# A six-block latent transformer on one core: the first group's order, products of zeros ahead of it, norms' deviations as powers on GpSimd, and two stores issued earlier

## Chip, core and metric

One core of a Trainium2 chip. The core has a matmul engine (TensorE, PE in the profile; its weight loads are PEld), VectorE (DVE), ScalarE (ACT), GpSimd (POOL) and SyncE (SP), which issues most DMAs. Each engine works through its own queue in order; semaphores tie the queues together. The metric is the device time of one launch in microseconds, the median of several runs. All data is float32.

## What is computed

There are 64 sequences of 32 tokens with 256 features, 2048 tokens in 16 tiles of 128, and a context of 257 rows of 64 features per sequence. Six blocks follow one another, each added to the residual:

```python
x = x + _L0_xattn_ref(_layernorm(x), ctx_512, Wq, Wkv_expand, Wout)   # causal, 16 heads of 16; the first 32 context rows matter
x = x + _L0_attn_ref(_layernorm(x), g_norm, Wq, Wkv, Wout, g_out)     # 16 heads of 128, one key head, l2-normed q and k
x = x + _L0_ffn_ref(_layernorm(x), Wr, br, W1, W2)                    # gelu, best 4 of 16 blocks of each token
x = x + _L1_xattn_ref(_layernorm(x), ctx_512, ...)                    # latent cross attention over 257 rotated keys
x = x + _L1_attn_ref(_layernorm(x), Wq, bq, Wk, bk, Wv, bv)           # causal, grouped keys
x = x + _L1_ffn_ref(_layernorm(x), router_w, gate_w, up_w, down_w)    # best one of 8 experts
```

A layer norm is `(x - mean) / sqrt(var + 1e-5)`. The kernel needs `1 / sqrt(var + eps)` for each token, and the second block has a norm of a norm.

## The kernel before

The residual stays on the chip in 16 tiles `xs[t]`; four tiles make a group `g`, and most projections are done for a group (512 columns) at a time. The six blocks are six stages with pools of their own, which reuse one another's space on the chip, so a buffer of a new stage can have to wait until the old stage's last readers, DMAs among them, are done. The stages are named a to f. In every stage PE's order is the program's order (`manual_schedule`); in stage b this holds for DVE, ACT and POOL too, in stage c for ACT. Where an engine is not listed, a planner with a cost model sets its order by when it thinks the operands are ready, and SyncE's DMA issues are ordered by the planner throughout.

**Norms.** `stats` (L141) takes mean and variance on DVE. `rstd_of` (L131) makes the reciprocal deviation in three steps: add eps on DVE (L134), square root on ACT (L136), reciprocal on DVE (L138). `ln_group` (L146) does four tiles; with `twice` it calls `rstd_of` a second time for the norm of a norm; it ends with the shift (L161) and the scaling of the four tiles, on DVE (L171) or ACT (L167). Square root belongs to another function table of ACT than exp or gelu, so a load of a table stands wherever the kind changes. Names of norms: a, b, r and c (the routing and the hidden layer of the third block), d, e, f (the last block's routing, `route_norm`, L1533).

**The start of stage a.** SyncE issues the constants (L72: 1214 columns, among them the identity for turning tiles, two masks, and at the end cosines and sines of the rotation), then the tiles 0 to 3 of x, the weights of a, the context of group 0, further x and contexts, then the weights of later stages. `group(g, part)` (L347) makes the features of a group in three parts: part 0 norms and turns the latents (`transposed`), part 1 makes the queries, part 2 the keys from the context (`ctxa`, L369), which ACT writes in four masked copies (L377). For group 0 the parts run in the order 2, 0, 1 (L445), then `score(0)` (L384). For tiles t = 0 to 17 the loop at L457 then runs the scores of t + 1, the output of t - 2, the values of t + 1 and so on, with one part of the next group per tile.

**Stage b** goes tile by tile; on every second t, `rotate` (L624) rotates a tile of the context on POOL and stores it for stage d. `rotate_last` (L654) does so for the last, 257th, key of all sequences: five small loads, three products and sums on POOL, and a store to `lkd` (L671). It stands at t = NT = 16, the loop's last turn (L913).

**Stage c** computes the hidden layer (`hidden`, L558, gelu on ACT; `output`, L572) of groups 1 to 3, and between them merges the weights of the fourth block. In its last group, each of four steps i does an output tile, a part of stage d's first queries (`d_queries`, L1047), and `last_out(i)` (L1019), which computes the last key's part of the output, copies it to `zs`, which lies in the space of the weight d_q, and after each second call stores half of it to `zd` with two DMAs (L1031). Products of `d_queries` and `last_out` share two PSUM buffers ("w").

**Stage d** starts with `score(0)`: PE (L1235), maximum on DVE (L1243, `nm`), exp on ACT (L1247, into `pp`), product on DVE (L1256). Its pool reuses the space of stage c's weights.

**Stage e** runs per tile: scores on PE (L262), mask and maximum on DVE, subtraction on POOL (L217), exp on ACT, turn on PE (L230), values spread on POOL (`vde`, L1498), output on PE (L1510), x added on POOL (L1524). The norms of groups e2 and e3 and the five norms of the routing f lie in it, and POOL also stores the rows of each expert (L1615). **Stage f** then computes 23 tiles of expert rows.

Of the kernel before, what the change touches and what calls it, by code (L numbers as in the profile page):

```python
# [7 lines left out]
F32 = mybir.dt.float32  # L8
# [5 lines left out]
P = 128  # L14
# [31 lines left out]
def perceiver_kernel(ctx: ExitStack, tc: tile.TileContext, a: dict, out: bass.AP):  # L46
# [17 lines left out]
    def weight(pool, name, shape):  # L64
        return pool.tile(shape, F32, name=name)
# [3 lines left out]


    cst = const.tile([P, C_N], F32, name="cst")
    nc.sync.dma_start(cst, a["consts"])  # L72
    xf = [const.tile([P, DP], F32, tag=f"x{t}", name=f"x{t}") for t in range(NT)]
    xs = [x[:, :D] for x in xf]
    for t in range(4):
        nc.sync.dma_start(xs[t], a["x"][t * P : (t + 1) * P, :])
    a_q = weight(wap, "a_q", [P, KC, D])

    a_kv = weight(wap, "a_kv", [P, 2 * D])
# [28 lines left out]
        nc.sync.dma_start(xs[t], a["x"][t * P : (t + 1) * P, :])  # L108
    for g in range(1, NG):
        load_ctxa(g)  # L110

    ident = cst[:, C_ID : C_ID + P]
    blk = cst[:, C_BLK : C_BLK + P]
# [8 lines left out]
    srt = dram.tile([NR, DP], F32, name="srt")  # L122
    ones = const.tile([P, S], F32, name="ones")
    nc.vector.memset(ones, 1.0)
    qeps = const.tile([P, 1], F32, name="qeps")
    nc.vector.memset(qeps, 1e-12 / 4096.0)
    keps = const.tile([P, 1], F32, name="keps")
    nc.vector.memset(keps, 1e-12 / 16.0)


    def rstd_of(mv, n, name):  # L131

        ve = sm(f"lnv_{name}", [P, n])
        nc.vector.tensor_scalar_add(ve, mv[:, :, 1], EPS)  # L134
        sd = sm(f"lns_{name}", [P, n])
        nc.scalar.activation(sd, ve, AF.Sqrt)  # L136
        rs = sm(f"lnr_{name}", [P, n])
        nc.vector.reciprocal(rs, sd)  # L138
        return rs
# [3 lines left out]
        nc.vector.bn_stats(st, src)  # L143
        nc.vector.bn_aggr(mv_slot, st)

    def ln_group(g, name, twice=False, act=False):  # L146

        mv = sm(f"lnm_{name}{g}", [P, 4, 2])
        for i in range(4):
            stats(mv[:, i, :], xs[4 * g + i], f"{name}{g}_{i}")  # L150
        rs = rstd_of(mv, 4, f"{name}{g}")
        if twice:

            v2 = sm(f"lnw_{name}{g}", [P, 4, 2])
            nc.vector.tensor_tensor(v2[:, :, 1], mv[:, :, 1], rs, ALU.mult)
            nc.vector.tensor_tensor(v2[:, :, 1], v2[:, :, 1], rs, ALU.mult)
            rs2 = rstd_of(v2, 4, f"{name}{g}b")
            nc.vector.tensor_tensor(rs2, rs2, rs, ALU.mult)
            rs = rs2
        sh = sm(f"lnh_{name}{g}", [P, 4])  # L160
        nc.vector.scalar_tensor_tensor(sh, mv[:, :, 0], -1.0, rs, ALU.mult, ALU.mult)  # L161
        xn = []
        for i in range(4):
            y = xnp.tile([P, D], F32, tag="xn", name=f"xn_{name}{g}_{i}")
            x_ = xs[4 * g + i]
            if act:
                nc.scalar.activation(  # L167
                    y, x_, AF.Identity, scale=rs[:, i : i + 1], bias=sh[:, i : i + 1]
                )
            else:  # L170
                nc.vector.scalar_tensor_tensor(  # L171
                    y,
                    x_,
                    rs[:, i : i + 1],
                    sh[:, i : i + 1].to_broadcast([P, D]),
                    ALU.mult,
                    ALU.add,
                )
            xn.append(y)
        return xn  # L180
# [98 lines left out]
    kvp = wb0.enter_context(tc.tile_pool(name="wB0", bufs=2))  # L279

    def keys_norm(g):
        latT[g] = ln_group(g, "b", twice=True, act=True)

    def keys_turn(g, ps):
        latT[g] = transposed(latT[g], ps, g, "b", gain=gn)
# [41 lines left out]
    with tc.tile_pool(name="wA", bufs=2) as work, tc.tile_pool(  # L327
# [19 lines left out]
        def group(g, part):  # L347

            if g >= NG:
                return  # L350
            if g not in feats:
                qT = work.tile([P, KC, 512], F32, tag="qT", name=f"qTa{g}")
                kd = work.tile([P, KC, 16, 2, S], F32, tag="kd", name=f"kda{g}")
                feats[g] = [qT, kd, None]
            if part == 0:
                feats[g][2] = transposed(ln_group(g, "a"), ps2, g, "a")
            qT, kd, xT = feats[g]
            for o in range(KC):
                osl = slice(o * P, (o + 1) * P)
                if part == 1:  # L360
                    q_ps = ps2.tile([P, 512], F32, tag="mm", name=f"qa{g}_{o}")
                    for k in range(KC):
                        nc.tensor.matmul(
                            q_ps, a_q[:, k, osl], xT[:, k, :], start=(k == 0), stop=(k == KC - 1)
                        )
                    nc.scalar.copy(qT[:, o, :], q_ps)
                if part == 2:
                    k_ps = ps2.tile([P, 512], F32, tag="mm", name=f"ka{g}_{o}")
                    nc.tensor.matmul(  # L369
                        k_ps,  # L370
                        a_kv[0:DC, osl],
                        ctxa[0:DC, 4 * g : 4 * g + 4, :],
                        start=True,
                        stop=True,
                    )
                    for w in range(2):
                        nc.scalar.activation(  # L377
                            kd[:, o, :, w, :],
                            k_ps.rearrange("p (b k) -> p b k", b=16),
                            AF.Copy,  # L380
                            scale=mask2[:, w : w + 1],
                        )
# [59 lines left out]
                )  # L442
            nc.vector.tensor_add(xs[t], xs[t], y_ps)

        for part in (2, 0, 1):  # L445
            group(0, part)
        score(0)
        values(0)
# [195 lines left out]
    with tc.tile_pool(name="wB", bufs=2) as work, tc.tile_pool(  # L644
# [229 lines left out]
        for t in range(NT + 1):  # L874


            parts = [AHEAD + 4 * t + z for z in range(4)]

            def place(z):
                if z < 4:  # L880
                    query_part(parts[z])
                for step in steps.get((t, z), ()):
                    step()

            if t < NT:
                similar(t)
            place(0)
            if t > 0:
                gather(t - 1)
            if t < NT:  # L890
                scale(t)
            place(1)
            square(t + 1)
            ff_late()
            place(2)
            if t < NT:
                power(t)
            ff_late()
            place(5)
            if t > 0:  # L900
                project(t - 1)
                norm_stats(t - 1)
            if t < NT:
                share(t)
            place(3)
            ff_late()
            if t > 0:
                norm_out(t - 1)
            if t % 2 == 0 and t < NT:
                rotate(t // 2, work)  # L910
                if t // 2 + 1 < NT // 2:
                    fetch(t // 2 + 1, work)
            if t == NT:  # L913
                rotate_last()
            place(4)
        for step in steps.get((NT + 1, 2), ()):
# [11 lines left out]
    with tc.tile_pool(name="wC", bufs=2) as work, tc.tile_pool(  # L928
# [151 lines left out]
        for g in range(1, NG):  # L1080
# [3 lines left out]
                hidden(g, f, xT, mb[f], hs[f], ps2, "h")()  # L1084
            if g == 1:
                mb = spread(2)
                xn = ln_group(2, "c")
            if g == 2:
                choose_blocks(3, ps2, work)
                choose_best(3, work, range(4))  # L1090
            if g == 3:
                xn = ln_group(0, "d")
            if g == 3:
                last_load()
            for step in chains.get((g, 0), ()):
# [3 lines left out]
            for i in range(4):  # L1099
                output(g, hs, i, ps2, "y")  # L1100
                if (g, i) == (1, 1):
                    xT = transposed(xn, ps2, 2, "c")
                    choose_norm(3, act=False)
                if (g, i) == (1, 3):
                    xT_c3 = choose_turn(3, ps2, work)
                if (g, i) == (2, 2):
                    choose_store(3, ps2, work)
                if g == 3 and i == 0:
                    latT[0] = transposed(xn, ps2, 0, "d")
                    queries[0] = w1.tile([P, 8, 8, S], F32, tag="t1", name="qTd0")  # L1110
                if g == 3:
                    d_queries(0, i, ps2, "w")
                    last_out(i)
            if g == 2:
                xT = xT_c3
                mb = spread(3)
# [6 lines left out]
    with mbw, wd1:  # L1123
# [3 lines left out]
        with tc.tile_pool(name="wD", bufs=2) as work, tc.tile_pool(  # L1127
# [200 lines left out]
            steps, lat = {}, {}  # L1328
            for g in range(1, NG):
                b0 = 16 * (g - 1)  # L1330
                steps[b0 + 1] = lambda g=g: lat.update({g: ln_group(g, "d")})

                def half(k, g=g):
                    if k == 0:
                        latT[g] = xtp.tile([P, KC, 512], F32, tag="xT", name=f"xT_d{g}")
                    transposed_part(lat[g], latT[g], ps1, k, f"d{g}")

                steps[b0 + 3] = lambda half=half: half(0)
                steps[b0 + 7] = lambda half=half: half(1)
            steps[48] = lambda: lat.update(e=ln_group(0, "e"))  # L1340
            steps[50] = lambda: e_group_start(0)
            steps[61] = lambda: lat.update(e1=ln_group(1, "e"))
            for z, b_ in enumerate((51, 55, 56, 58, 59, 60)):
                steps[b_] = lambda z=z: (
                    transposed_part(lat["e"], feats[0][2], ps1, z, "e0")
# [110 lines left out]
    with tc.tile_pool(name="wE", bufs=2) as work, tc.tile_pool(  # L1456
# [7 lines left out]
        def group(g, part):  # L1464
# [8 lines left out]
                for o in range(KC):  # L1473
                    e_features(g, part, o, ps2)
            if part == 3 and g + 1 < NG:
                lat[g + 1] = ln_group(g + 1, "e")

        def score(t):
            g, i = divmod(t, 4)
# [53 lines left out]
        def route_norm(ts):  # L1533
            n_ = len(ts)
            mv = sm(f"lnq_f{ts[0]}", [P, n_, 2])
            for i, t in enumerate(ts):
                nc.gpsimd.tensor_copy(mv[:, i, :], rows[t][:, 0, :])
            rs = rstd_of(mv, n_, f"f{ts[0]}")
            sh = sm(f"lnh_f{ts[0]}", [P, n_])
            nc.vector.scalar_tensor_tensor(sh, mv[:, :, 0], -1.0, rs, ALU.mult, ALU.mult)  # L1540
            rows[ts] = []
# [334 lines left out]
```

## Time and profile before

| | |
|---|---|
| median of 3 runs | 1316.46 us (1315.89 to 1319.39) |
| the profiled execution's own time | 1319.55 us |
| its span, first to last instruction | 1317.8 us |
| mean granted TensorE clock | 0.941 |
| function table loads of ACT | 1.283 us each |
| stage a, from the first latents' norm | 5.07 us |
| stage c, first product of the hidden layer | 514.31 us |
| stage d, first scores | 649.32 us |
| stage e, first scores | 1006.00 us |
| stage f, first expert rows | 1170.95 us |

Times in the profile count from the start of the span. A line of the timeline is: start, length, engine, line of the kernel, operation, output<-input, how many; in brackets the engine's idle time before it and what ended it. A busy row gives busy microseconds, share of the span and number of instructions. The slices are 40 equal parts of the span with the busy share in tenths. A float32 product is written as two records. "Waits" lists who waited for whom. A wait for several things is named after the one that came last in the profile, which can be a bystander.

### The profile page before, as it was taken

To read this page: it belongs to the slowest core of one execution; us is meant where nothing else is said; L and a number is where in the kernel's file an instruction comes from. 1 tells how busy PE (TensorE), PEld (TensorE's weight loads), DVE (VectorE), ACT (ScalarE), POOL (GpSimd) and SP (SyncE) were. 2 spreads that over 40 slices of the span, in tenths; PEclk is the share of its full clock that TensorE was granted. 3 is DMA by queue.
4 is the path that set the end of the run, shared out by engine and by line. 5 is a ranking of instruction groups with operands and counts; after the bars stand their busy time and mean duration, and the time that the engine had idled before them with its cause. 6 is when DMAs were issued, how large, how long until landed. Compare 5 with 4: busy or idle time off the path is not lost. (4 is left out here: it accounts for less than half of the span.)

```text
span 1317.8 us, 25995 instructions
## 1 busy us (share of the span) xinstructions
PE 1188.5 (90%) x10153; PEld 830.1 (63%) x10153; DVE 779.7 (59%) x1786; ACT 567.8 (43%) x1292; POOL 367.1 (28%) x468
## 2 busy tenths in 40 slices
PE   5888999999999998999789998999997687669997
PEld 2555767777776665786666766777765465436664
DVE  6665246778767775433388787777674465434343
ACT  3345353464553641213255565656563354311111
POOL 1222243455443521000055252000002456621111
PEclk9999899999999989979999998999999788669999
DMA  8990110111121212802254442112004600011110
GB/s 256 308 326 6 27 41 1 40 41 41 42 73 33 81 41 81 232 1 66 57 155 105 105 131 58 46 36 53 27 1 160 226 3 19 18 49 45 34 46 18
DMA packets 94443, 103.08 MB, mean 78 GB/s; under 512 B 37648, under 2 KB 71057, under 8 KB 93842
## 3 DMA queue, kind: packets, MB, share of 16 engines
q1 hardware_dynamic: 92450, 97.19, 25.6%
q0 software_dynamic: 1872, 4.23, 0.9%
q8 instruction: 81, 1.33, 0.4%
q14 instruction: 40, 0.33, 0.1%
HBM read 69.45 MB, written 32.85 MB: 78 GB/s over the span
## 5 line engine op out<-in xcount | busy, mean ns | idle before, releaser
L1247 ACT ACTIVATE pp<-Sd,nm 128x257 f32<-128x257 f32 x256 | 118.2, 475 | 71.0 <-DVE nm L1243 66.4
L693 PE MATMUL qb<-xT_b,b_q 128*128 128x256 f32 x512 | 124.0, 391 | 0.0
L693 PEld LDWEIGHTS qb<-xT_b,b_q 128*128 128x128 f32 x512 | 96.4, 193 | 39.7 <-issue 19.6
L784 PE MATMUL yb<-b_o,oTb 128*128 128x256 f32 x512 | 116.0, 386 | 0.0
L784 PEld LDWEIGHTS yb<-b_o,oTb 128*128 128x128 f32 x512 | 98.3, 194 | 14.3 <-issue 0.7
L1256 DVE TENSOR_TENSOR pp<-pp,rd 128x514 f32<-128x514 f32 x128 | 101.9, 796 | 2.2
L1243 DVE TENSOR_REDUCE nm<-Sd 128x2 f32<-128x514 f32 x128 | 82.8, 684 | 20.4 <-PE Sd L1235 20.3
L1278 ACT COPY pTd<-pt 128x512 f32<-128x512 f32 x112 | 61.4, 598 | 51.9 <-PE pt L1272 51.9
L628 POOL TENSOR_TENSOR rct<-rct,cst 128x514 f32<-128x514 f32 x16 | 21.0, 1311 | 209.3 <-DMA rrt<-in_ctxT_dram 191.1
L1295 PE MATMUL od<-pTd,na 128*64 128x256 f32 x480 | 66.4, 397 | 9.8 <-issue 7.3
L712 POOL TENSOR_TENSOR q2b<-qTb 128x512 f32<-128x512 f32 x64 | 65.2, 1049 | 30.0 <-ACT qTb L701 17.3
L1235 PE MATMUL Sd<-ct,qTd 64*128 64x257 f32 x480 | 70.4, 407 | 2.2 <-ACT pp L1247 2.1
L701 ACT COPY qTb<-qb 128x512 f32<-128x512 f32 x64 | 37.4, 585 | 72.3 <-PE qb L693 70.7
L1272 PE MATMUL pt<-cst,pp 128*128 128x128 f32 x512 | 67.0, 274 | 0.0
L1272 PEld LDWEIGHTS pt<-cst,pp 128*128 128x128 f32 x512 | 59.3, 141 | 10.1 <-issue 5.8
L1055 PE MATMUL qd<-xT_d,d_m 128*128 128x256 f32 x256 | 65.3, 399 | 0.2 <-ACT xT_d L192 0.2
L803 POOL TENSOR_TENSOR ynb<-ynb,vec 128x256 f32<-128x256 f32 x16 | 11.6, 727 | 192.1 <-DVE ynb L802 192.1
L746 DVE RECIPROCAL rqb<-rqb 128x512 f32<-128x512 f32 x16 | 53.5, 3343 | 17.8 <-ACT rqb L741 17.8
L575 PE MATMUL yc<-c,hc 128*128 128x256 f32 x256 | 60.4, 393 | 2.7 <-DVE hc L570 2.7
L1311 PE MATMUL yd<-d_n,co 128*128 128x256 f32 x256 | 61.3, 394 | 0.0
L1055 PEld LDWEIGHTS qd<-xT_d,d_m 128*128 128x128 f32 x256 | 47.2, 194 | 17.2 <-issue 6.0
L575 PEld LDWEIGHTS yc<-c,hc 128*128 128x128 f32 x256 | 49.9, 197 | 12.4 <-DVE hc L570 3.5
(360 smaller groups left out, 2405.0 us busy)
## 6 DMA issues: line engine op xcount, KB each, us to landing
srt<-pad SPq DMA_DIRECT2D x17, 1040.0 KB
mb<-maskd SPq DMA_DIRECT2D x64, 128.0 KB
ct<-ctd SPq DMA_DIRECT2D x30, 257.0 KB
rct<-in_ctxT_dram SPq DMA_DIRECT2D x32, 128.5 KB
rrt<-in_ctxT_dram SPq DMA_DIRECT2D x64, 64.2 KB
ctd<-rct SPq DMA_DIRECT2D x32, 128.5 KB
nad<-rna SPq DMA_DIRECT2D x16, 256.0 KB
fw<-in_f_wg_dram SPq DMA_DIRECT2D x8, 512.0 KB
```

Source lines behind the costliest of these rows:

```text
L575: nc.tensor.matmul(y_ps, hs[f][:, i * P : (i + 1) * P], c_2[:, f, :], start=(f == 0), stop=(f == 7),)
L693: nc.tensor.matmul(q_ps[:, hh, :], b_q[:, k, h * P : (h + 1) * P], xT[:, k, c0 : c0 + 256], start=(k == 0), stop=(k == KC - 1),)
L712: nc.gpsimd.tensor_tensor(q2[:, 4 * h4 : 4 * h4 + 4, :], q, q, ALU.mult)
L784: nc.tensor.matmul(y_ps, oT[:, h, :], b_o[:, h, :], start=(h == 0), stop=(h == NH - 1))
L1055: nc.tensor.matmul(q_ps[:, r, :], m[:, k, pr * P : (pr + 1) * P], xT[:, k, c0 : c0 + 256], start=(k == 0), stop=(k == KC - 1),)
L1235: nc.tensor.matmul(s_ps[:, hh, :NKV], qT[hs, b % 8, 4 * u : 4 * u + 4, :], ct[hs, b % 4, :], start=True, stop=True,)
L1243: nc.vector.tensor_reduce(nm, s_ps[:, :, :NKV], AX.X, ALU.max, negate=True)
L1247: nc.scalar.activation(pp[:, hh, :], s_ps[:, hh, :NKV], AF.Exp, bias=nm[:, hh : hh + 1], accum_out=sd[:, hh : hh + 1],)
L1256: nc.vector.tensor_tensor(pp, pp, bc(rd, 2, NKV), ALU.mult)
L1272: nc.tensor.transpose(pt[:, hh * 256 + u * P : hh * 256 + u * P + P], probs[b][:, u, hh, c * P : (c + 1) * P], ident,)
L1278: nc.scalar.copy(pT[:, c, :], pt)
L1295: nc.tensor.matmul(o_ps[64 * hh : 64 * hh + 64, 0, :], na[:, j, c, :], pT[:, c, hh * 256 : (hh + 1) * 256], start=(c == 0), stop=(c == 1),)
```

## The change

Constants: columns from the cosines on are loaded later; x of tiles 0 to 3 is issued first. The parts of group 0 run as 0, 1, 2, and 18 products of zeros (128x128 by 128x256, from the zero tile `pad` into a buffer nobody reads) are issued on PE ahead of them. `rstd_of` gets a second form: add eps and raise to the power -0.5, both on GpSimd; it is used for all a norms, b of group 0 (both times), c of group 2, d of groups 0 and 3, all e and all f norms. `rotate_last` moves from t = 16 to t = 13. `last_out` 0 and 1 are called at i = 0, and 2 and 3 at i = 1.

```diff
     cst = const.tile([P, C_N], F32, name="cst")
-    nc.sync.dma_start(cst, a["consts"])
...
     for t in range(4):
         nc.sync.dma_start(xs[t], a["x"][t * P : (t + 1) * P, :])
+
+    nc.sync.dma_start(cst[:, :C_COST], a["consts"][:, :C_COST])
...
     for g in range(1, NG):
         load_ctxa(g)
+    nc.sync.dma_start(cst[:, C_COST:], a["consts"][:, C_COST:])
...
+    mhalf = const.tile([P, 4], F32, name="mhalf")
+    nc.vector.memset(mhalf, -0.5)
...
-    def rstd_of(mv, n, name):
+    def rstd_of(mv, n, name, power=False):
+
+        if power:
+            rs = sm(f"lnr_{name}", [P, n])
+            nc.gpsimd.tensor_scalar(rs, mv[:, :, 1], EPS, None, ALU.add)
+            nc.gpsimd.tensor_tensor(rs, rs, mhalf[:, 0:n], ALU.pow)
+            return rs
...
-        latT[g] = ln_group(g, "b", twice=True, act=True)
+        latT[g] = ln_group(g, "b", twice=True, act=True, power=g == 0)
...
-                feats[g][2] = transposed(ln_group(g, "a"), ps2, g, "a")
+                feats[g][2] = transposed(ln_group(g, "a", power=True), ps2, g, "a")
...
-        for part in (2, 0, 1):
+        warm = ps2.tile([P, 256], F32, tag="mm", name="warm")
+        for _ in range(18):
+            nc.tensor.matmul(warm, pad[:, 0:P], pad[:, 0:256], start=True, stop=True)
+        for part in (0, 1, 2):
             group(0, part)
...
-            if t == NT:
+            if t == NT - 3:
                 rotate_last()
...
-                xn = ln_group(2, "c")
+                xn = ln_group(2, "c", power=True)
...
-                xn = ln_group(0, "d")
+                xn = ln_group(0, "d", power=True)
...
                     d_queries(0, i, ps2, "w")
-                    last_out(i)
+                    for r2 in ((0, 1), (2, 3), (), ())[i]:
+                        last_out(r2)
...
-                steps[b0 + 1] = lambda g=g: lat.update({g: ln_group(g, "d")})
+                steps[b0 + 1] = lambda g=g: lat.update({g: ln_group(g, "d", power=g == 3)})
...
-            steps[48] = lambda: lat.update(e=ln_group(0, "e"))
+            steps[48] = lambda: lat.update(e=ln_group(0, "e", power=True))
-            steps[61] = lambda: lat.update(e1=ln_group(1, "e"))
+            steps[61] = lambda: lat.update(e1=ln_group(1, "e", power=True))
...
-                lat[g + 1] = ln_group(g + 1, "e")
+                lat[g + 1] = ln_group(g + 1, "e", power=True)
...
-            rs = rstd_of(mv, n_, f"f{ts[0]}")
+            rs = rstd_of(mv, n_, f"f{ts[0]}", True)
```

## The prediction

> **What bounds the kernel now.** I read the page first. The share rows and the slices:
>
> ```profile
> span 1317.8 us, 25995 instructions
> ...
> PE 1188.5 (90%) x10153; PEld 830.1 (63%) x10153; DVE 779.7 (59%) x1786; ACT 567.8 (43%) x1292; POOL 367.1 (28%) x468
> ...
> PE   5888999999999998999789998999997687669997
> ...
> PEclk9999899999999989979999998999999788669999
> ```
>
> PE is busy for 90%, so the kernel is a chain of PE stages and what can be won is PE idle time, and PE time at a low clock. The chain of waits covers only the last 90 us (the stores of the last stage), where PE is full anyway. So I went to the waits of PE, then to busy time by windows around the dips:
>
> ```profile
> 514.00:520.00 6.00, 3.67 (x8) 1.44 (x8) 4.33 (x22) 1.69 (x2) 1.96 (x5) 1.00 0.14 34
> 520.00:524.00 4.00, 3.76 (x5) 1.70 (x6) 1.29 (x2) 0.80 (x3) 0.00 (x0) 0.57 1.03 348
> ...
> 650.00:657.00 7.00, 0.46 (x6) 0.05 (x2) 2.85 (x11) 1.84 (x4) 0.00 (x0) 0.73 0.68 113
> 657.00:664.00 7.00, 6.48 (x23) 4.59 (x24) 4.97 (x12) 3.91 (x17) 0.00 (x0) 0.54 0.57 149
> ...
> 1046.00:1056.00 10.00, 3.82 (x107) 2.50 (x108) 7.53 (x17) 4.51 (x6) 7.42 (x12) 0.83 0.01 2
> ```
>
> Columns: length, busy us of PE, PEld, DVE, ACT, POOL, granted clock, DMA share. Twice a hole in PE is followed by a stretch at 0.54 to 0.57 of the clock: a hole costs its length and then some. The timeline names who holds PE in each (start, length):
>
> ```profile
> 11.77 3.75 PE L369 MATMUL ka<-ctxa,a_kv 64*128 64x512 f32 x4 [11.77 <-DMA ctxa<-in_ctxa_dram]
> ...
> 17.79 5.58 PE L363 MATMUL qa<-xT_a,a_q 128*128 128x512 f32 x8
> ...
> 24.04 0.41 PE L262 MATMUL S_a<-kda,qTa 32*32 32x64 f32 x32 [0.35 <-ACT qTa L366]
> ...
> 516.15 0.46 SPq L671 DMA_DIRECT2D lkd<-last  x1
> ...
> 518.29 1.28 ACT L569 ACT_TABLE_LOAD   x1 [5.79 <-DVE lnm_d L144]
> ...
> 519.59 1.08 ACT L569 ACTIVATE hc<-hp 128x512 f32<-128x512 f32 x2
> ...
> 520.24 12.18 PE L562 MATMUL hp<-xT_c,c 128*128 128x512 f32 x24 [2.26 <-ACT hc L569]
> ...
> 651.12 1.13 SPq L1031 DMA_DIRECT2D zd<-d_q  x2
> ...
> 655.15 1.28 ACT L1247 ACT_TABLE_LOAD   x1 [5.88 <-DMA zd<-d_q]
> ...
> 657.52 2.14 PE L1235 MATMUL Sd<-ct_d,qTd 64*128 64x257 f32 x8 [7.06 <-ACT pp L1247]
> ...
> 1053.49 0.47 PE L200 MATMUL tp_e<-cst,xn_e 128*128 128x128 f32 x1 [5.34 <-DVE xn_e L171]
> ```
>
> Four places, then: the start; the stage changes at 514 and 650, where ACT waits for a store from buffers that the next stage's pool reuses (at 518 the named DVE is a bystander: SyncE's next load, L935, is released at 518.03 by the DMA lkd<-last); and the norm of latent group 2 in the last attention.
>
> **The start.** Now: keys' projection 11.77, first latents turned 15.45, queries from 17.79, first scores done at 24.45. Query records stand 0.85 us apart until about 21.3 and 0.43 after, so nearly all this runs at half pace (the clock row says 1.00 here; I go by the pace). The change puts 18 products of zeros ahead, two records each: 36 records at 0.242 (L693: 124.0/512) are 8.7 us, at half pace (0.47, eight L1055 records in 3.78 at 659.59) 17. They can start at 1.4, after the memset of pad (0.87 to 1.15). With C us slow they take C + 0.242 x (36 - C/0.47) = 8.7 + 0.485 C. For C the rows give 3.1 (dense restart, 520.24 to 523.3), about 5.6 (657.5 to 663) and 9.5 (11.77 to 21.3, with pauses). The Trainium skill ("TensorE: Matmul & The Clock Gate", Part 1: The HAM clock gate) says that the clock follows activity in free-running windows of about 3.4 us: C between 3.4 and 6.8 for a dense start, and more products than fill this only occupy the array. By the rule the zeros end at 11.8 to 13.4, by the paused row at 14.7. They are dense, so I take C = 4.5, end at 12.3.
>
> The turns queue behind the zeros on PE, and their norm is ready sooner: x now goes ahead of the constants on SyncE. Should DVE keep mask2 and caus4 first, these wait for the constants, now fifth, where the last x was (stats from 5.07): xn at about 10, as before (9.85). The zeros cover that too; without them it would cost 2. So the zeros are the bound. From their end, at full pace: the turns (0.66 each, copies 0.59) to +1.95, the queries, begun on the first half at +1.4, to +4.9 (3.67 for eight records at 70.71), the keys (1.98 at 78.85) to +6.6, their four masked copies of 0.63 from +5.85 to +8.35, scores +8.8: 21.1. Gain 3.3 (2.2 to 3.8 by the rule, an estimate; 0.9 with C = 9.5). The masked copies used to hide under the queries; that is in the sum. Zeros might not count as activity at all: 1.4 + 17, then all at half pace, scores at about 31: minus 7. The second half of the constants is one more issue, 0.5 us on SyncE, ahead of b_q, first read at 150: nothing; cos and sin are first read near 160.
>
> **Store of the last key's row (L671).** At t = 13, 50 us earlier. Its five loads were already issued at 158. Its three POOL steps (0.31 each) then stand ahead of q2b of tile 15; POOL idles 14.9 us there (before 467.52): nothing. What is late next is the store maskd<-mTc (L548, issued 514.19; 1.9 us as L671 took, so 516.1). Table 1.28, gelu at 517.4 instead of 519.59: 2.2; PE gets the buffers at 518.0, just as it ends its second block, so the 2.26 hole closes and the half pace to 523.3 (1.5 lost) probably with it. Taken 3.0, from 1.5 (idling since 511.5 still throttles) to 4.
>
> **Store zd (L1031).** Parts 2 and 3 move up two steps of i (12 us): issued near 640 and landed by 644 (4.0 after issue, as 651.12 to 655.15), ahead of e_q (646.08) in SyncE's queue. PE's sum is the same; the two buffers of "w" suffice (qd copied at 630.28, when the second zp begins). Next late is nm, ready 650.9. Exp starts between 651.0 (table loaded while waiting) and 652.3, not 656.44: 4.2 to 5.4. The hole in PE shrinks from 7.1 to 1.5-3, so the half pace from 657.5 (eight L1055 records 3.78, against 1.99 at 759.40) should go: 1.9, part of it hidden by DVE. Taken 6.0, from 4 to 7.5; 0 if the store stays behind e_q.
>
> **Norms on GpSimd.** Eighteen pairs add + power replace add, Sqrt, reciprocal. No row has a power; the nearest is:
>
> ```profile
> L1379 POOL TENSOR_TENSOR e_bk<-e_b,mask 128x4 f32<-128x4 f32 x1 | 0.2, 203 | 2.4 <-DMA e_b<-in_vecs_dram 2.4
> ```
>
> So the add is 0.2, the power at least 0.2; for the top I give its four elements per partition fifty times the 2 ns of a 128x512 product (L217, 1049 ns): 0.6. I take 0.3, for its nearness to the row. The Trainium skill speaks against it ("GPSIMD Engine Reference", 2.1 Instruction dispatch): a freshly loaded kernel pays about 6 us at its first call. That would put xn at about 15 and the scores at 24, and erase the start's gain. But the first tensor_tensor here (26.12) took 1.04, as the mean, with no gap, and the power is the same instruction: I take no load.
>
> What falls away: about 19 table loads of 1.283 us. Most lie beside PE work. Groups a and b0 (xn_b is needed 20 us later), c2 and d3: nothing. d0: its load holds the copies of n (PE waits 0.80 and 0.38 at 620-623), but groups 1 and 2 still need Sqrt there: 0.3 of 0 to 1.2. e0, e1: 2.77 of ACT each, PE waits under 1.1 and 0.3 behind: 0.6.
>
> Last attention: at 1047 ACT loads Sqrt, waits for DVE until 1050.03, and the reciprocal stands behind the next tile's softmax on DVE (1051.62). With POOL the power follows vde (ends 1048.63), by 1049.2 to 1050; DVE's shift waits for it, and behind it the tile's s_e and mx. PE's 5.3 us shrink by 2 to 3, and some of the half pace to 1061 goes: 3.0. The routing's end: xn_f of tiles 12 to 14 starts at 1150.45, held by reciprocals that sit behind rank; with powers about 1149.1: 1.3. Against it POOL, 62 to 69% busy from 1060 to 1140, carries 0.5 more per norm, seven times, and softmax waits on it after the row stores (1096.88, 1130.56): minus 1.0. Sum 3.3, from 0 to 8.
>
> **Sum.** 3.3 + 3.0 + 6.0 + 0.3 + 0.6 + 3.3 = 16.5. The stages between are full PE (20.00 of 20 in most windows), so shifts pass through. The profiled execution took 1319.55 (span 1317.8 and 1.75 around it): 1303.0. The median of the runs lies 3.1 lower: 1300.
>
> **Rivals.**
> - The start gives nothing or costs 7 (zeros too long, or not lifting the clock). For: the 9.5 row. Against: both dense rows. 1303 to 1310. Chance 0.17.
> - Another release takes the stores' place: the pool waits for mTc's store later than I think, and the second zd store stays behind e_q. For: SyncE issued zd behind seven e_q/e_k loads. Against: the first pair went ahead of e_q at 637.2. 9.0 falls to about 2: 1307. Chance 0.12.
> - More in the last attention: the loads held DVE and POOL in turn, and the clock (0.50 to 0.83 there) recovers: 6 to 8 more, 1293. For: the 3.8 busy of 10. Against: POOL's load. Chance 0.15.
> - Slower: the power is long, T us, in POOL's in-order queue. Seven norms in the last attention and one at the start pay it: 8T against 16.5, level at T = 2.1; at 2.8 it gives 1322. For: nothing but the missing row. Chance 0.04.
> - Otherwise as forecast, 1296 to 1305: 0.52.
>
> A measurement of this kernel tells 0.3%, about 4 us, from no change: 1312.5 and 1320.4 are the bounds. Faster 0.92, same 0.04, slower 0.04. Range 1291 to 1310.
>
> **What would show it.** First scores at 21 with query records 0.43 apart; gelu at 517 less the shift, with its next releaser the mTc store; exp within 2 us of nm at the third change; tp_e of group 2 under 3 us late; powers of 0.3. I am wrong if the zeros run at 0.47 to their end, if ACT again waits for a store at either change, or if powers exceed 1 us.

## The result and the profile after

The changed kernel takes 1299.82 us, the median of 4 runs (1294.96 to 1301.94). The kernel before, on the same chip, takes 1316.78 (1315.89 to 1319.39). The ratio is 0.9863, interval 0.9829 to 0.9896: 13.7 to 22.5 us less. The forecast was 1300.0. The profiled execution took 1298.15.

The head of its page, with the busy row, and the slices of PE and of the granted clock:

```profile
span 1296.4 us, 26028 instructions
...
PE 1187.8 (92%) x10189; PEld 833.3 (64%) x10189; DVE 769.0 (59%) x1751; ACT 540.1 (42%) x1255; POOL 389.7 (30%) x504
...
PE   6898999999999999999989999999998687669997
...
PEclk8889999999999989979999989999999788669999
```

PE's busy time is what it was (1188.5 before), but 10.0 us of it are now zeros, which fill a part of the first hole. The real products are busy for 10.8 us less, and the rest of the gain is holes that closed: about half each. The first slice holds zeros, and behind it the clock falls, as it does not in the kernel before. The row of the clock counts a stretch without a record as full: the first record stands at 5.3 us here and at 21.8 in the kernel before, whose products ran at half pace until then.

The changed kernel's timeline, lines that answer to those shown of before:

```profile
1.19 10.04 PE L457 MATMUL warm<-pad 128*128 128x256 f32 x36 [1.19 <-DVE mhalf L128]
11.07 1.04 PE L197 MATMUL tp_a<-cst,xn_a 128*128 128x128 f32 x8
12.35 3.70 PE L372 MATMUL qa<-xT_a,a_q 128*128 128x512 f32 x8 [0.24 <-ACT xT_a L201]
...
19.61 0.41 PE L271 MATMUL S_a<-kda,qTa 32*32 32x64 f32 x32 [0.75 <-ACT kda L386]
...
23.78 0.16 DVE L170 SCALAR_TENSOR_TENSOR lnh_a<-lnm_a,lnr_a 128x4 f32<-128x4 f32 x1 [1.16 <-POOL lnr_a L140]
...
25.36 1.04 POOL L140 TENSOR_TENSOR lnr_a<-lnr_a,mhalf 128x4 f32<-128x4 f32 x1
26.43 0.16 DVE L170 SCALAR_TENSOR_TENSOR lnh_a<-lnm_a,lnr_a 128x4 f32<-128x4 f32 x1 [1.47 <-POOL lnr_a L140]
26.51 0.68 DVE L216 SCALAR_TENSOR_TENSOR s_a<-S_a,caus 128x512 f32<-128x512 f32 x1
27.25 1.10 PE L271 MATMUL S_a<-kda,qTa 32*32 32x64 f32 x64 [6.12 <-DVE s_a L216]
...
518.10 1.28 ACT L582 ACT_TABLE_LOAD   x1 [5.15 <-DMA maskd<-mTc]
519.39 1.08 ACT L582 ACTIVATE hc<-hp 128x512 f32<-128x512 f32 x2
...
520.04 10.57 PE L575 MATMUL hp<-xT_c,c 128*128 128x512 f32 x24 [1.62 <-ACT hc L582]
...
649.01 0.48 ACT L1261 ACTIVATE pp<-Sd,nm 128x257 f32<-128x257 f32 x1 [1.10 <-DVE nm L1257]
```

Four things are to be seen.
- The first scores are done at 20.02 (19.61 + 0.41), 4.4 us sooner than before. Tile 0's softmax, the first product that DVE makes of them, starts at 26.51, where before it started at 24.62: norms of later groups stand ahead of it in DVE's queue, and two of them wait for a power of 1.04 us (1.16 and 1.47 us of idle time). PE, which needs the scores' buffer, waits 6.12 us. The lead is gone.
- Gelu of stage c starts at 519.39, only 0.20 sooner. In this execution ACT now waits for the store of the block mask (mTc).
- Exp of stage d waits for the maximum and no longer for a store: 2.35 us after the first scores (646.66), where it was 7.12.
- A power of 128x4 takes 1.04 us and the add ahead of it 0.23; 128x1 takes 0.58.

Where the two profiled executions part, by the start of a step in each (from the timelines):

| step | before | after | gained in the stretch |
|---|---|---|---|
| first similarity of stage b | 166.54 | 166.89 | -0.35 |
| first product of the hidden layer, stage c | 514.31 | 514.74 | -0.08 |
| first scores of stage d | 649.32 | 646.66 | 3.09 |
| last output of stage d | 1004.89 | 991.56 | 10.67 |
| first expert rows, stage f | 1170.95 | 1149.59 | 8.03 |
| end of the span | 1317.8 | 1296.4 | 0.04 |

These are one execution of each. The six kernels with the old start reach stage b between 162.9 and 168.9, so the first two rows lie within what executions differ by. The sum is 21.4; the runs' medians are 17.0 apart, since the profiled execution of before (1319.55) lies above its median and that of after (1298.15) below its own. The start shows no gain here, and stages d and e give 18.7 where some 10 were forecast.

### The profile page after: what moved, and what is told of

It reads as the page before. It is cut to its first block, busy times and chain, and to the rows that moved or that the text cites. A ratio compares the mean times of both kernels' runs of the same rounds, so it can differ in the third digit from the quotient of the medians.

```text
span 1296.4 us, 26028 instructions
## 1 busy us (share of the span) xinstructions
PE 1187.8 (92%) x10189; PEld 833.3 (64%) x10189; DVE 769.0 (59%) x1751; ACT 540.1 (42%) x1255; POOL 389.7 (30%) x504
## 3 DMA queue, kind: packets, MB, share of 16 engines
q8 instruction: 82, 1.34, 0.4%
## 5 line engine op out<-in xcount | busy, mean ns | idle before, releaser
L1270 DVE TENSOR_TENSOR pp<-pp,rd 128x514 f32<-128x514 f32 x128 | 98.4, 769 | 2.1
L1292 ACT COPY pTd<-pt 128x512 f32<-128x512 f32 x112 | 61.5, 599 | 52.1 <-PE pt L1286 52.1
L1765 POOL DMA_INDIRECT out_dram<-os,ti x23 | 22.7, 986 | 124.4 <-DVE os L1762 100.8
L773 DVE RECIPROCAL rdb<-denb 128x512 f32<-128x512 f32 x16 | 53.7, 3355 | 5.8 <-PE denb L771 5.6
```

The costliest lines, as they stand in the source:

```text
L1270: nc.vector.tensor_tensor(pp, pp, bc(rd, 2, NKV), ALU.mult)
L1292: nc.scalar.copy(pT[:, c, :], pt)
```

## The experiments

The theory after this comparison: the start's lead is eaten in DVE's queue, by norms whose powers take 1.04 us, and the late stages gain by powers. The rivals: the powers cost nothing there, or the lead is lost further on; and what the late stages gain is not the powers'.

All were timed against the kernel before, in three sets on three chips. The kernel before has medians of 1317.45, 1316.85 and 1317.65 there, but its single runs go from 1308.4 to 1325.3, so what one change is worth is taken from the ratio, times 1317, and not from two medians. Kernels with fewer than 10 runs have wide intervals.

| kernel | us | ratio | interval | less than before, us |
|---|---|---|---|---|
| start with roots | 1313.04 | 0.9974 | 0.9958 to 0.9991 | 1.2 to 5.5 |
| start with powers | 1313.01 | 0.9969 | 0.9953 to 0.9986 | 1.8 to 6.2 |
| store lkd alone | 1313.29 | 0.9980 | 0.9964 to 0.9996 | 0.5 to 4.7 |
| store zd alone | 1308.67 | 0.9928 | 0.9904 to 0.9952 | 6.3 to 12.6 |
| both stores | 1305.01 | 0.9907 | 0.9874 to 0.9940 | 7.9 to 16.6 |
| powers of e alone | 1312.60 | 0.9957 | 0.9941 to 0.9974 | 3.4 to 7.8 |
| powers of c to f | 1308.02 | 0.9933 | 0.9915 to 0.9951 | 6.5 to 11.2 |
| all, without zeros | 1303.84 | 0.9903 | 0.9868 to 0.9937 | 8.3 to 17.4 |
| all, roots in a1 to a3 | 1297.52 | 0.9838 | 0.9809 to 0.9867 | 17.5 to 25.2 |
| all, DVE's order by hand | 1315.51 | 0.9983 | 0.9970 to 0.9997 | 0.4 to 4.0 |
| all, mask early | 1300.39 | 0.9893 | 0.9856 to 0.9930 | 9.2 to 19.0 |
| mask early, roots in a and b | 1294.51 | 0.9851 | 0.9816 to 0.9886 | 15.0 to 24.2 |

**The start alone, with roots** (`start_only`):

```diff
 for part in (2, 0, 1)                     ->  zeros; for part in (0, 1, 2)
 cst, then x                               ->  x, then cst[:, :C_COST]
 transposed(ln_group(g, "a"), ...)             (roots, as before)
```

> The kernel before with only the start of the change: x ahead of the constants, products of zeros, latents ahead of keys. All norms keep their roots and both stores stay where they were. Theory 1 (VectorE's queue): tile 0's softmax stands behind norms of groups 1 and 2 in VectorE's order, whatever their form, so it starts near 24 us, where it started before (24.62), although its scores are done near 20: PE then has a hole of about 4 us and the start gives 0 to 1.5 us, 1315 to 1316.5. Theory 2 (the powers alone take the lead away): with roots the softmax follows its scores at 20 to 21 us and the start gives 3.3 to 4.4 us, 1312 to 1313.

Softmax of tile 0 followed its scores at 21.88, and the ratio gives 3.4 us, both near what theory 2 said. But the profile doesn't show the gain at the start: the first output of stage a is at 44.09 (43.46 before) and stage b's first similarity at 165.33 (166.54), 1.2 sooner. So the lead is lost by 44 us even where no softmax stands behind a power. Busy time and clock from 22 to 45 us, before, here and in the changed kernel (PE, PEld, DVE, ACT and POOL busy, clock, DMA share, GB/s):

```profile
22.00:45.00 23.00, 18.21 (x436) 10.83 (x442) 14.84 (x40) 7.78 (x15) 6.24 (x6) 0.93 0.90 310
22.00:45.00 23.00, 18.25 (x336) 10.71 (x319) 13.79 (x35) 9.20 (x14) 6.30 (x6) 0.74 0.90 310
22.00:45.00 23.00, 16.27 (x316) 9.71 (x316) 15.60 (x41) 5.51 (x10) 8.85 (x10) 0.70 0.91 313
```

PE is as busy here as before and gets through 100 records less. The granted clock of this stretch is 0.85 to 0.93 in the six kernels with the old start and 0.69 to 0.81 in the eight with the new one. The first output comes at 42.3 to 43.5 in those six, and in the new order, DVE's order by hand left aside, at 42.6 to 44.1 in six kernels and 40.3 in one.

**The start alone, with powers** (`start_powers`): as above, with `power=True` for a and for b of group 0.

> The kernel before with the start of the change and the powers of stages a and b, no other powers and no stores moved. The start with roots took 1313.04 where before took 1317.45. Theory 1 (the powers of 1.04 us ahead of tile 0's softmax in VectorE's queue eat the start): softmax at 26 to 26.5 us again, and nothing is left of the gain: 1316 to 1318. Rival (the powers cost next to nothing there, and the lead of the changed kernel was lost to a run's clock): 1312 to 1313.

The softmax went back to 26.16, as theory 1 had it, and the time did not change: 1313.01 against 1313.04. Theory 1 has the place of the stall right and its worth wrong. Stage b's first similarity is at 169.06, 3.7 later than with roots; that is one execution of each (`best1` below, with the same roots in stage a, reaches it at 160.11), and the timed runs don't carry it. In neither profile does the gain of about 4 us lie in the start.

**Roots back in the changed kernel** (`a_roots`):

```diff
-ln_group(g, "a", power=True)
+ln_group(g, "a", power=g == 0)
```

> The changed kernel with the norms of groups 1 to 3 of stage a on roots again (group 0 keeps its power). Theory 1 (VectorE's queue): these norms still stand ahead of tile 0's softmax, only their waits are shorter; it starts near 25 us instead of 26.51, worth 1 to 1.5 us: 1298 to 1299. Theory 2 (the powers alone): softmax near 21 us, 4 us or more regained: 1295.5 or less.

Softmax at 22.92; 1297.52, an interval that overlaps the changed kernel's. It settles nothing between 1 and 4 us.

**DVE's order by hand** (`hand_order`): stage a's order of DVE is the program's.

```diff
-tc.manual_schedule(engines={PE})
+tc.manual_schedule(engines={PE, DVE})
 score(t + 1); project(t - 2); values(t + 1)
+finish(t + 1)      # sum, reciprocal and product, taken out of score
```

> The changed kernel with VectorE in the program's order in stage a, each tile's sum of exponentials put behind the next products of values so that the order does not stall; norms of groups 1 to 3 then come behind tile 0's softmax. Powers stay. Theory 1 (VectorE's queue): softmax of tile 0 at 20 to 20.5 us instead of 26.51, PE's hole of 6.1 us goes, and 4 to 6 us are gained: 1294 to 1296. Rival (stage a is bound further on by VectorE or by the loads, so the lead is lost there): within 1 us of 1299.8, or slower where the fixed order stalls.

The rival. Softmax started at 20.85, the soonest of all, and the kernel lost nearly everything. Among who waited for whom, and in the timeline:

```profile
PE tp_a L197 <- DVE xn_a L180: 15.6, 3, 6.6
```

```profile
33.52 2.43 PE L197 MATMUL tp_a<-cst,xn_a 128*128 128x128 f32 x8 [6.55 <-DVE xn_a L180]
```

In program order a group's norm comes just ahead of its turn on PE, and three turns wait 15.6 us in all. The norms that the planner put too early at tile 0 were early for a reason.

**Without the zeros** (`no_zeros`): the 18 products taken out of the changed kernel.

> The changed kernel without the products of zeros. PE then comes cold to the turns and the queries: they run at half pace for 3 to 4 us, so the first scores come 3 to 4 us later, at 22 instead of 18.45. Theory 1: that is hidden, since tile 0's softmax stands behind norms until 26.5 in VectorE's queue anyway: 1299 to 1301. Rival (the scores' time counts): 3 us more, 1303.

The time is 1303.84; its interval overlaps the changed kernel's. Its start:

```profile
7.69 2.52 PE L197 MATMUL tp_a<-cst,xn_a 128*128 128x128 f32 x8 [7.69 <-DVE xn_a L180]
10.03 5.93 PE L372 MATMUL qa<-xT_a,a_q 128*128 128x512 f32 x8
...
19.52 0.41 PE L271 MATMUL S_a<-kda,qTa 32*32 32x64 f32 x32 [0.75 <-ACT kda L386]
```

The queries are slow (5.93 against 3.70), but the turns start when the norm is ready, at 7.69 rather than 11.07, where they had stood behind zeros. Scores are done at 19.93 without zeros and 20.02 with them. My expectation of 3 to 4 us later was wrong, and theory 1's reason for a small difference isn't the one: at the start the zeros cost just what they give. What they do give lies 1000 us later; see below.

**The two stores** (`stores_only`): only `rotate_last` at NT - 3 and `last_out` 0 to 3 in the first two steps.

> The kernel before with only the two stores moved (last key's rotation at tile 13, its output's stores in the first two steps). By the prediction's sum 9.0 us: 1307.5. By the trace of the changed kernel, where gelu still begins at 519.39 behind the block mask's store: about 2.2 for the first store (half of it only a clock at full pace) and 5.7 for the second, 7.9 in all: 1308.6. If the first store is worth nothing because the mask's store takes its place: 1310.8.

1305.01, 2.5 us under the sum of the prediction; by the ratio 12.2 us, and its interval, 7.9 to 16.6, holds the 9.0.

**The first store** (`lkd_only`) and **the second** (`zd_only`), each alone:

> The kernel before with only the last key's rotation and store moved to tile 13. By the prediction's sum 3.0 us less: 1314.5. If the block mask's store, issued at 514.6 and waited for until 518.1, simply takes its place: 0 to 0.5 us less, 1317. The stores together gave 12.4 us; if the second gives what its stage shows (5.7), the first gives 6.7 and this kernel takes 1310.8, which would need a cause that the prediction lacks.

> The kernel before with only the last key's output moved to the first two steps of stage c's last group. By the prediction's sum 6.0 us less, 1310.8: exp of stage d's first block within 2 us of its maximum, where before it waited 7 us for a store. By the two runs with stores (12.4 both, 2.6 to 3.6 the first) 9 to 10 us: 1307.5, for which stage d would have to stay shorter after the first block too. If another release takes the store's place: under 2 us.

The first agrees with 3.0; the second gave 9.5, and 6.0 lies just outside its interval. In the traces, gelu starts 5.2 to 5.4 us after the stage's first product where the store lkd is in place, and 4.11, 3.40, 4.65, 4.96 and 3.40 where it was moved with the mask's store left as it was (lkd alone, both, the changed kernel, roots back, no zeros). The 3.40 are what is left when no store is waited for (next experiment), so the mask's store took the place in some executions and not in others. Exp of stage d starts 7.1 to 7.4 us after the first scores where zd is in place and 2.3 to 2.8 where it was moved.

**The mask's store out of the way** (`mask_early`):

```diff
-at(4 * g + 8, 5, choose_best(g, work, (2, 3)));  at(4 * g + 9, 2, choose_store(g))
+at(4 * g + (7 if g == 2 else 8), 5, ...);        at(4 * g + (8 if g == 2 else 9), 2, ...)
```

> The changed kernel with the last two rounds of choosing blocks for group 2 one tile earlier, and the store of its mask ahead of the last output of stage b instead of behind it. If the mask's store is what the first gelu of stage c waits for (518.1), gelu then follows its products and the last copies out of stage b's buffers: at 515 to 516 instead of 519.39, 3 to 3.5 us less, 1296.5. If another late release stands behind it (last norm of stage b, table load of gelu), 1 us or less: 1299.

The time did not move. ACT's line of the timeline says why:

```profile
517.40 1.28 ACT L582 ACT_TABLE_LOAD   x1 [3.32 <-PE hp L575]
```

With no store left, gelu waits for its own products. It starts 3.39 us after the first of them, against 4.65 in the changed kernel: 1.26 was all there was to have, not 3 to 3.5. I had left out the 1.7 us that the products take, and the table load.

**Early mask and roots in a and b together** (`best1`):

> The changed kernel with roots again in the norms of stages a and b, and the mask's store early as in the run before this one. With roots tile 0's softmax started at 21.88 (26.51 with powers). If both gains hold and add up: 2.3 to 4 us for the start and 3 for the mask, 1293 to 1294.5. If the start's gain is lost again before stage b: 1296.5.

1294.51, the lowest median of all, and the number expected, but not for the reason: the mask alone had given nothing, and by the ratio roots back in a1 to a3 stand lower (0.9838). The interval overlaps the changed kernel's, so it beats the kernel before but not, by these runs, the changed one.

**The powers of stages c to f** (`late_powers`) and **of e alone** (`e_powers`):

> The kernel before with only the powers of stages c to f (c of group 2, d of groups 0 and 3, all e, all f); start, stores and the norms of a and b as before. By the prediction's sum 4.2 us less (d 0.3, e0 and e1 0.6, the rest 3.3): 1313.2. By the one profile of the changed kernel, which shows stages d to f 12.9 us shorter from 655 us on: 1304.5. If those 12.9 us are mostly from elsewhere (a planner's order, a run's clock), as a look at stage e of kernels with the same roots suggests (158 to 166 us from the last output of stage d to the first expert rows): 1312 to 1314.

> The kernel before with only the four powers of stage e's norms. All powers of stages c to f gave 8.8 us. By the prediction's sum 3.6 of its 4.2 are e's (e0 and e1 0.6, e2 3.0): 1313.5. By the traces: the wait for e2's norm of 5.34 us goes, and 0.87 us for each of e0 and e1 in stage d, 7 us: 1310. If it is the routing's norms that give most: 1314 or more.

8.8 us, twice the 4.2 of the prediction's sum, and 5.7 for e alone. That is less than the 12.9 that the one profile suggested, so something else gains there too.

**What the zeros do in stage e.** The wait of group 2's turn (tp_e) for its norm is 5.34, 5.72, 5.22 and 5.35 in the four kernels with roots in e and no zeros, 3.59 to 3.80 with powers and no zeros, 1.25 and 1.43 with roots and zeros, and under 0.5 with both. Zeros at 1 us thus shorten a wait at 1053. Two timelines of stage e, first the kernel before, then the changed one, show the link:

```profile
1016.12 0.35 PE L262 MATMUL S_e<-kde,qTe 32*32 32x64 f32 x18
1020.22 0.94 PE L262 MATMUL S_e<-kde,qTe 32*32 32x64 f32 x46 [3.75 <-issue]
1021.09 1.94 PE L1487 MATMUL ve<-e_v,xT_e 128*32 128x64 f32 x64
1022.96 1.12 PE L230 MATMUL ptp_e<-cst,s_e 128*128 128x128 f32 x4
1024.00 0.65 PE L1510 MATMUL oe<-vde,pT_e 128*32 128x64 f32 x14
1026.69 0.85 PE L1510 MATMUL oe<-vde,pT_e 128*32 128x64 f32 x18 [2.04 <-issue]
```

```profile
1007.75 0.53 PE L1501 MATMUL ve<-e_v,xT_e 128*32 128x64 f32 x20 [3.02 <-issue]
1008.21 0.66 PE L239 MATMUL ptp_e<-cst,s_e 128*128 128x128 f32 x4
1008.80 1.08 PE L1524 MATMUL oe<-vde,pT_e 128*32 128x64 f32 x32
1009.81 1.10 PE L271 MATMUL S_e<-kde,qTe 32*32 32x64 f32 x64
1010.83 0.44 PE L1501 MATMUL ve<-e_v,xT_e 128*32 128x64 f32 x8
1013.78 1.72 PE L1501 MATMUL ve<-e_v,xT_e 128*32 128x64 f32 x56 [2.50 <-issue]
```

"issue" is a stall for which the timeline names nothing. From one to the next are 46 + 64 + 4 + 14 = 128 records before, and 20 + 4 + 32 + 64 + 8 = 128 after; each record has a weight load on PEld, so 256 instructions. The same count stands between such holes in every kernel here: 127 or 128, or about twice that where one fell into longer products (a few such sums are off by up to 14, as records can be missing or listed twice). Counted from the start of the program, the first of these holes stands behind record 7125 to 7127 in all seven kernels without zeros, and behind 7253 to 7255, 128 more, in all seven with them. The 36 records of zeros move all later block ends by 36 places: in the kernels without zeros the holes lie in S_e, oe, ve and S_e, in those with zeros in ve, ve, oe and ve. The kernel without zeros, which else is the changed one, has them where the kernel before has them:

```profile
1007.15 0.71 PE L271 MATMUL S_e<-kde,qTe 32*32 32x64 f32 x48 [2.21 <-issue]
...
1013.06 0.53 PE L1520 MATMUL oe<-vde,pT_e 128*32 128x64 f32 x20 [1.71 <-issue]
...
1019.26 0.85 PE L1497 MATMUL ve<-e_v,xT_e 128*32 128x64 f32 x20 [3.75 <-issue]
```

The traces do hold a sign of what PE waits for. One DMA queue, q8, brings instructions: 82 packets in 1.34 MB in the changed kernel, and PE's 10189 records with as many loads make about 80 times 256. The three longest holes of the changed kernel's stage e (the ones ended at 1007.75, 1013.78 and 1027.86) hold one packet of it each (packets, MB, share of the DMA engines' time):

```profile
q8 instruction: 1, 0.02, 2.0%
q8 instruction: 1, 0.02, 2.4%
q8 instruction: 1, 0.02, 2.2%
```

All 50 such holes of 0.9 us or more between the last output of stage d and that turn, in all 14 kernels, end 1.2 to 1.6 us after such a packet has landed. So PE waits there for its own instructions. Why they come so late isn't shown.

The holes ahead of that turn add up to much the same (8.2 to 11.0 us without zeros, 8.2 to 10.3 with). My reading is that with zeros the last of them, in ve behind the scores, falls into time that PE would have spent waiting for the norm. From the last output of stage d to group 2's queries it is 52.1 to 56.0 us in the seven kernels without zeros and 47.7 to 49.8 in the others. A table from the last output of stage d to the first expert rows, means of the executions of each kind:

| | roots in e and f | powers in e and f |
|---|---|---|
| without zeros | 164.4 (4: 161.0 to 166.8) | 159.8 (2: 159.6, 160.0) |
| with zeros | 160.1 (2: 159.9, 160.4) | 156.4 (5: 155.5 to 158.0) |

So zeros are worth 4.3 or 3.4 us there and powers 4.6 or 3.7; the left column's ranges nearly touch, the right one's do not. It is the size of the gain, about 4 us, that the two kernels with only the start have. That the place of the holes does it, and no other effect of the zeros, is argued from these records: a kernel with as many instructions added elsewhere on PE wasn't run.

## Why the prediction was right, and where it wasn't

The total was right, but not by its steps. One by one:

- **Start, 3.3.** The working up to the first scores holds: they were done at 20.02 (21.1 forecast). The zeros doubled their pace 4.0 us after the first (4.0 to 5.7 in the seven kernels with zeros, inside the 3.4 to 6.8 by the prediction's rule), where I had C = 4.5; what was off is the time of a zero record at full pace, 0.216 and not 0.242, so they ended at 11.2 and not 12.3:

```profile
1.19:5.19 4.00, 4.00 (x10) 3.19 (x10) 1.00 0.73 187
5.19:11.07 5.88, 5.88 (x28) 4.99 (x26) 1.00 0.50 100
```

  The step that failed is the one not written: that scores sooner mean everything sooner. "The stages between are full PE, so shifts pass through" does not hold for the start of stage a, where PE of the kernel before is busy for 18.21 of 23 us. It did not look at DVE's queue, in which two waits for powers (1.16 and 1.47 us) and the norms of three groups stood ahead of tile 0's softmax. Nor did it look at the clock: with roots the softmax was not held up, and the lead was lost all the same, at a granted clock of 0.74 from 22 to 45 us where it had been 0.93. How much each of the two took isn't shown. And the zeros were no gain at all there, since the turns waited for them from 8.9 (norm done) to 11.07.
- **A term that was missing, 3.4 to 4.3.** The zeros' 72 instructions shift PE's holes in stage e. It stood in for the start's 3.3 in the sum by chance.
- **Store lkd, 3.0.** Mechanism as written, in this execution: the next releaser was the mask's store. It was estimated to land at 516.1 and was waited for until 518.1 (issued 514.62, 0.43 later than in the kernel before; the landing varies between executions). PE's second run of products went at full pace (24 records in 10.57), as forecast. Alone 2.6, 0.5 to 4.7.
- **Store zd, 6.0.** Exp started 2.35 us after the scores, not 7.12. From first scores to last output of stage d it is 355.9 us on the mean of five kernels with zd in place and roots in d, and 349.7 of the two with zd moved (347.6 and 351.8): 6.2. Right, as far as two executions carry it. The timed 9.5 alone has more in it than this stage shows; that stays open.
- **d0, 0.3, and e0, e1, 0.6.** Small and too small: from the products np (L1012) to the first scores of stage d it was 31.2 to 31.4 in the kernels with a root there and 30.3 or 30.4 in those with a power, 0.8 to 1.1; e1's two table loads cost 0.87 by themselves (between outputs 8 and 9 of stage d, 21.44 before, 20.57 in the changed kernel). e0's part can't be read for holes of "issue" beside it.
- **Last attention and routing, 3.3.** The powers there gave 4.6 and 3.7 by the table; with the others of c to f 8.8 in time. Mis-sized, low.
- **The power itself.** 0.3 was taken with a top of 0.6; it is 1.04 for four elements per partition and 0.58 for one, so the bound was wrong too: the row of e_bk was near in shape but not in kind. By "if powers exceed 1 us" I should have been wrong, at 8 T = 8.3 us. I was not, because the price of 8 T assumed that each power lay on the path: they replace loads and roots of the same length, and start_powers takes what start_only takes. No first call cost anything beyond that: the first power took 1.06. A second of my signs of being wrong came true, that ACT again waits for a store at a change (at 518.10, for mTc). It contradicts the sentence before it, which names that store as the next releaser.

The rivals: the start gave nothing by the first output of stage a (the first rival), for reasons not named there; another release took the first store's place (the second), worth 1.26 us at the most; and stages d and e gave more (the third). All three came in part, and their sizes cancelled. The parts measured alone (start 4.1, stores 12.2, late powers 8.8) add up to 25.1, the whole gives 18.0 (13.7 to 22.5). Some is counted twice, as zeros and powers shorten the same wait; whether that is all, these intervals can't tell.

## What to carry to other kernels

An operand that is ready sooner helps only if its consumer stands next in its own queue: before crediting a lead, list what is ahead of the consumer on that engine, and what each of those waits for. Then compare the granted clock of the stretch behind it, since a lead can be spent there too. Where a step is bounded by the nearest row, near must mean the same operation; two engines' times for an add say nothing of a power. And a total that comes true is no proof of its terms: here a lead that was lost and a gain nobody aimed at were of one size, and only runs of each part alone showed it.

## What the hardware did that I had not expected

- PE stalls for up to 4.4 us at the ends of blocks of 256 of its instructions where these are short (stage e: 13 to 20 ns per record). The Trainium skill ("Runtime: NRT & Kernel Launch", Instruction fetch mechanics) says that instructions come in blocks of 256 and that the cost of crossing from one to the next is mostly hidden. The count agrees with the holes and the packets here; the cost does not: 8 to 11 us ahead of group 2's turn alone.
- After the zeros the clock does not stay up. In the changed kernel the granted clock is 0.62 from 20 to 30 us and 0.70 from 30 to 40, where PE waits 6 us for the softmax; in the kernel before it is 1.00 and 0.83 there. The zeros are not what lowers it: without them, the rest as changed, it is 0.74 and 0.75. The changed kernel:

```profile
20.00:30.00 10.00, 3.31 (x107) 1.69 (x104) 6.50 (x24) 0.63 (x1) 3.58 (x5) 0.62 0.85 303
30.00:40.00 10.00, 9.09 (x169) 6.20 (x170) 9.25 (x21) 2.33 (x4) 4.15 (x4) 0.70 1.07 371
```

 The columns of this view by windows are PE, PEld, DVE, ACT and POOL busy, clock, DMA share and GB/s.
- Zeros count as work: the pace of PE doubled after 4.0 us of zeros, while the real products of the same kernel without zeros, from 7.69 on, came to full pace at 14.5.
